# Convolution-attention hybrid, two layers: edge columns of a key-table group in one transfer, other ring sizes, new order offsets

## The chip, the cores and the metric

The kernel runs on one core of a Trainium2 chip. The core has TensorE (PE), whose weight loads are listed apart (PEld), VectorE (DVE), ScalarE (ACT), GpSimd (POOL), and SyncE (SP), which here only issues DMA transfers. The metric is the time of one execution on the device, in microseconds; smaller is better. Three runs of the kernel before took 1271.53 to 1274.23 us, with a median of 1273.8 us.

## The reference, cut to what matters

The input x has 2 images of 256 channels and 48x48 pixels. The first layer is a mixture of local attention and dynamic convolution:

```python
x = x + L0_conv(_gn(x))          # _gn: group norm
# in L0_conv, per image and per head (4 heads of 64 channels):
q = (Wq x + bq) * 64**-0.5 ; k = Wk x + bk ; v = Wv x + bv
uk, uv, upe = unfold 7x7 of k, v, pe, each padded by 3 with mode='reflect'
att = softmax(einsum('bdn,bdkn->bnk', q, uk + upe))
out_att = einsum('bnk,bdkn->bdn', att, uv)
# and two 3x3 depthwise convolutions with a relu between them
return rate1 * out_att + rate2 * out_conv
```

So each pixel attends to the 7x7 pixels around it, and at the border of the image the neighbours are reflected. The second layer (a state-space mixer and eight experts, two per token) follows on the same pixels as tokens. The change does not touch it.

## The kernel before, in words

Layer 0 runs for both images as one stream of work, and the second layer begins when it is done.

**Attention in blocks.** An image is cut into 18 blocks of 8x16 queries (`QR`, `QC`), six rows of three columns, 36 blocks in both images. A block needs the 14x22 keys around it (`KR`, `KC`, 308 in all). Its steps, with the lines of the profile: scores on PE (L811), mask and minimum on DVE (L827), exponentials on ACT (L838), transposes of the probabilities on PE (L846), their copy on ACT into a `pt` tile (L852), and the mix with the values on PE (L868). Beside that, DVE takes the inverse of each softmax sum (`rden`, L884). POOL widens it to a tile `rx` of 128x256 (L889), PE transposes that (L894), ACT copies the result from PSUM into a tile `rb` (L900), and DVE multiplies the mix with it (`ot`, L882, called norm here) and adds it to x (L878).

**Values through memory.** The values are computed in pairs of 128 pixels, nine pairs per image: product on PE (L749), copy on ACT into a `vout` tile (L756), store to a raster in device memory (L759). When three pairs are there, that is 16 rows of the image, the group is spread into a table, `vtab`, by transfers from memory to memory: for each of the three columns of blocks a strip of 22 pixels per row (L769), whose reflected edge columns come one by one, three at the left edge of the first strip (L772) and three at the right edge of the last (L775). For the top and bottom of the image three reflected rows are copied within the table (L781, L783, called ends here). A block then loads its 308 values of 256 channels in three transfers into a `val` tile (L911). All of these, stores, spreads, ends and loads, are issued by SP in one queue, in the order of the program: an issue that waits holds up all that stand behind it.

**Convolution beside it.** The two depthwise convolutions run in strips of 24 rows: most taps are multiply-adds on DVE (L565, L577), some are products on ACT (L626) which POOL adds by accumulating transfers (L638).

**Who sets the order.** Class `Flow` plans layer 0 as a list: every step has an engine, a cost in ns, the steps that it needs, and the ring slots that it takes and frees (`room`: two `vout`, three `val`, two `rb`, two `rx`, and so on). A step's rank is its due time less the length of what follows, less an offset of its kind from the table `LEAD0` (a minus or a plus behind the name stands for the first or the second half). Whenever an engine is free, the ready step of lowest rank with free slots is taken. The order found is the order of the instructions of PE, DVE, ACT and SP; POOL's follows it. The costs in the code only make the order. The engines wait for semaphores when they run.

Of the kernel before, what the change touches and what calls it, by code (L numbers as in the profile page):

```python
# [38 lines left out]
B, C, H, W = 2, 256, 48, 48  # L39
# [3 lines left out]
PAD = 3  # L43
HP = H + 2 * PAD
QR, QC = 8, 16
# [4 lines left out]
NRB, NCB = H // QR, W // QC  # L50
# [182 lines left out]
class Kernel:  # L233
# [104 lines left out]
    def layer0(self, ctx):  # L338


        nc, ins = self.nc, self.ins
        self.ps, self.used_banks = self.pool("ps", 1, ctx, space=bass.MemoryType.PSUM), []
        wts = self.pool("l0w", 1, ctx)
        room = dict(bank=2, banks=3, q=2, prob=3, pt=4, val=3, vout=2, hid=2, place=2, ct=2, cg=2, rb=2, ot=1, rx=2)
        self.begin_flow(self.pool("att", 1, ctx), room, self.PACE0, self.LEAD0, NBQ * self.PACE0)
        self.xp = {(b, h): wts.tile([P, H, W], F32, name=f"xp{b}{h}") for b in range(B) for h in range(NH)}
        self.kp = [wts.tile([P, HP, HP], F32, name=f"kp{h}") for h in range(NH)]
        self.prepare(wts)
        self.scale_weights()
        for b in range(B):  # L350
            self.group_norm(b)
            for g in range(-(-H // KG)):
                self.keys(b, g)
            for rb in range(NRB):
                self.queries(b, rb)
            for pair in range(N // (2 * P)):
                self.values(b, pair)
            self.convolutions(b)
            for i in range(NBQ):
                self.block(b * NBQ + i)  # L360
        self.run_flow()
# [371 lines left out]
    def values(self, b, pair):  # L733


        nc, T, p0 = self.nc, self.tiles, 2 * P * pair
        flat = [self.xp[b, h].rearrange("p r c -> p (r c)") for h in range(NH)]
        raster, key = self.vraster[b], (b, pair)
        r1 = (p0 + 2 * P) // W
        done = (p0 + 2 * P) % (VR * W) == 0  # L740
        group = p0 // (VR * W)
        c = b * NBQ + NCB * next(rb for rb in range(NRB) if min(QR * rb + QR + PAD, H) > group * VR)

        def product():
            ps = self.bank_for(("v", key))
            for i in range(2):
                p = p0 + i * P
                for k in range(NH):
                    nc.tensor.matmul(  # L749
                        ps[:, i * C : (i + 1) * C], lhsT=flat[k][:, p : p + P], rhs=self.l0["Wv"][:, k, :],  # L750
                        start=k == 0, stop=k == NH - 1,
                    )

        def copy():
            out = self.large_tile("vout", key, [P, 2, C])
            nc.scalar.copy(out.rearrange("p i c -> p (i c)"), T["bank", ("v", key)])  # L756

        def store():
            nc.sync.dma_start(raster[p0 : p0 + 2 * P, :].rearrange("(i p) c -> p i c", p=P), T["vout", key])  # L759

        def spread():
            r0 = r1 - VR
            src = raster.rearrange("(r c) d -> r c d", c=W)
            strips = self.vtab[b].rearrange("s (r c) d -> s r c d", c=KC)
            rows = slice(PAD + r0, PAD + r1)
            for cb in range(NCB):
                c0, c1 = max(0, cb * QC - PAD), min(W, (cb + 1) * QC + PAD)
                at = c0 - (cb * QC - PAD)
                nc.sync.dma_start(strips[cb, rows, at : at + c1 - c0, :], src[r0:r1, c0:c1, :])  # L769
                for j in range(PAD):  # L770
                    if cb == 0:
                        nc.sync.dma_start(strips[cb, rows, j : j + 1, :], src[r0:r1, PAD - j : PAD - j + 1, :])  # L772
                    if cb == NCB - 1:
                        col = QC + PAD + j
                        nc.sync.dma_start(strips[cb, rows, col : col + 1, :], src[r0:r1, W - 2 - j : W - 1 - j, :])  # L775

        def ends():
            strips = self.vtab[b].rearrange("s (r c) d -> s r c d", c=KC)
            for j in range(PAD):
                if group == 0:  # L780
                    nc.sync.dma_start(strips[:, j], strips[:, 2 * PAD - j])  # L781
                if r1 == H:
                    nc.sync.dma_start(strips[:, PAD + H + j], strips[:, PAD + H - 2 - j])  # L783

        self.op(c, ("v", key), "PE", 1730, product, *self.normalized(b, p0 // W, r1), ("wv1", 0), takes=[("bank", ("v", key))])
        self.op(c, ("vc", key), "ACT", 570, copy, ("v", key), takes=[("vout", key)], uses=[("bank", ("v", key))])
        self.op(c, ("vs", key), "queue", 4500, store, ("vc", key), uses=[("vout", key)])
        if done:
            self.op(c, ("vt", (b, group)), "queue", 10000, spread, *[("vs", (b, p)) for p in range(pair - 2, pair + 1)])
            if group == 0 or r1 == H:  # L790
                self.op(c, ("ve", (b, group)), "queue", 5800, ends, ("vt", (b, group)))

    def block(self, c):
# [122 lines left out]

    PACE0 = 8517
    LEAD0 = {
        "Wk-": -2983844, "Wq-": -2364428, "Wv-": 1379269, "add+": 4672699, "add-": -218998,
        "bkp-": -329119, "bq8-": -347513, "bv1-": -2824447, "c1+": -2744499, "c1-": 604148,  # L920
        "c2+": -3568598, "c2-": -4067744, "c3+": -4192745, "c3-": 1206176, "ca+": -316981,
        "ca-": 1533923, "cd+": -6915146, "cd-": 3124390, "copy+": 5626139, "copy-": -1580149,
        "cp+": -1382670, "cp-": -1157911, "cst-": 2506359, "exps+": -3895413, "exps-": -4687265,
        "g2+": 3892042, "g2-": -3058028, "ga-": -6766507, "gneg-": 557252, "gs-": -9485502,
        "ka+": -2261356, "ka-": 4495797, "kb+": 754107, "kb-": 2128455, "kk+": -355426, "kk-":
        95965, "least+": -852851, "least-": -3615547, "line-": -4892590, "mix+": 3379755,
        "mix-": 5352508, "norm+": -2808328, "norm-": -848702, "place+": 2730989, "place-":
        4548299, "q+": 272749, "q-": 1258423, "qp+": -359879, "qp-": 5581, "rc+": -1347439,
        "rc-": 1599623, "rden+": -1647488, "rden-": -463776, "relu+": 7308982, "relu-": 4577314,
        "row-": -5624948, "rstd-": 3924930, "rt+": 965921, "rt-": -18691, "rx+": -6558515,  # L930
        "rx-": -3369941, "score+": 3504231, "score-": 2190083, "sw+": -848532, "turn+":
        -1205935, "turn-": 84883, "v+": 110806, "v-": 10811, "val+": 448065, "val-": 3685159,
        "vc+": -519738, "vc-": -124400, "ve+": 2263088, "ve-": -7064210, "vec-": -4450165,
        "vs+": -1985565, "vs-": -5738649, "vt+": 5333280, "vt-": 1460046, "w2r-": -7510221,
        "win-": 4743570, "winw+": -1186160, "woutc+": 774295, "woutd+": 1826874, "woute+":
        -6026117, "woutt+": -512791, "woutw+": -8672401, "wp-": -1208524, "wv1-": -2064644,
        "x-": -4900900, "xp-": -8007513,
    }


# [1485 lines left out]
```

## Time and profile before

| what | us |
|---|---|
| median of three runs | 1273.8 |
| the profiled execution, its own time | 1275.69 |
| its span | 1273.9 |
| PE busy in the span | 1205.9 |
| DVE, ACT, POOL busy | 897.5, 779.9, 612.7 |
| end of layer 0 (last residual add of a block) | 304.6 |
| in 0 to 306: PE, DVE, ACT, POOL busy | 271.2, 261.9, 235.1, 127.1 |
| in 0 to 306: share of DMA engines busy | 0.65 |

The span is the time from the first to the last recorded instruction of one profiled execution. Busy time is the union of the records of an engine; matmuls are pipelined and their ends are modelled, so that a busy PE need not be at its peak. In a timeline a row is a group of like instructions that follow one another, with the idle time before the first and what released it. Rows of SP (`SPq`) are the issues of transfers, not the transfers themselves.

### The profile page before, as it was taken

To read this page: it belongs to the slowest core of one execution; us is meant where nothing else is said; L and a number is where in the kernel's file an instruction comes from. 1 tells how busy PE (TensorE), PEld (TensorE's weight loads), DVE (VectorE), ACT (ScalarE), POOL (GpSimd) and SP (SyncE) were. 2 spreads that over 40 slices of the span, in tenths; PEclk is the share of its full clock that TensorE was granted. 3 is DMA by queue.
4 is the path that set the end of the run, shared out by engine and by line. 5 is a ranking of instruction groups with operands and counts; after the bars stand their busy time and mean duration, and the time that the engine had idled before them with its cause. 6 is when DMAs were issued, how large, how long until landed. Compare 5 with 4: busy or idle time off the path is not lost. (4 is left out here: it accounts for less than half of the span.)

```text
span 1273.9 us, 23367 instructions
## 1 busy us (share of the span) xinstructions
PE 1205.9 (95%) x8024; PEld 977.0 (77%) x8024; DVE 897.5 (70%) x2385; ACT 779.9 (61%) x1774; POOL 612.7 (48%) x773
## 2 busy tenths in 40 slices
PE   4989999997999999999999989999999999999995
PEld 2666675776667777777776878999999999999995
DVE  7966899997687988888888645655555655556442
ACT  2488887997889888789698633333333333334342
POOL 3761235524367789899899872121212122212220
PEclk9989999998899999999999999999999999999998
DMA  7678873651223334335454248667657667656756
GB/s 261 157 191 217 207 182 76 140 127 42 74 88 99 103 100 129 123 96 174 140 180 143 69 135 273 186 229 228 221 173 257 186 227 221 229 174 216 224 180 211
DMA packets 106733, 212.98 MB, mean 167 GB/s; under 512 B 11615, under 2 KB 83632, under 8 KB 101680
## 3 DMA queue, kind: packets, MB, share of 16 engines
q1 hardware_dynamic: 85488, 168.51, 38.8%
q0 software_dynamic: 19008, 38.62, 16.0%
q10 hardware_dynamic: 2116, 4.33, 1.0%
q8 instruction: 65, 1.06, 0.3%
q14 instruction: 56, 0.46, 0.1%
HBM read 154.24 MB, written 43.23 MB: 155 GB/s over the span
## 5 line engine op out<-in xcount | busy, mean ns | idle before, releaser
L2154 POOL DMA_INDIRECT acc<-ey,token x70 | 109.3, 1562 | 367.6 <-ACT ey L2153 310.5
L2144 PE MATMUL bank<-ext,wt 128*128 128x256 f32 (+1 forms) x1152 | 241.3, 368 | 0.0
L2148 ACT ACTIVATE hid<-bank,bt 128x256 f32<-128x256 f32 (+1 forms) x288 | 132.1, 460 | 171.3 <-PE bank L2144 166.5
L2144 PEld LDWEIGHTS bank<-ext,wt 128*128 128x128 f32 x1152 | 207.0, 190 | 25.0
L2187 PE MATMUL po<-ts,ss 128*128 128x128 f32 x768 | 96.2, 275 | 0.0
L975 PE MATMUL bank<-xn,win 128*128 128x387 f32 x240 | 93.2, 512 | 1.6 <-ACT t L1058 1.6
L1188 DVE SCALAR_TENSOR_TENSOR xc<-bank,vec,xc 128x384 f32<-128x384 f32 x144 | 86.5, 610 | 8.4 <-ACT xc L1177 8.1
L2187 PEld LDWEIGHTS po<-ts,ss 128*128 128x128 f32 x768 | 90.9, 192 | 0.0
L1404 ACT ACTIVATE mt<-mt,cum 128x128 f32<-128x128 f32 x288 | 87.7, 392 | 0.0
L1738 POOL DMA_INDIRECT xs<-u,rows x72 | 73.2, 1016 | 17.5 <-issue 15.1
L838 ACT ACTIVATE prob<-prob,top 128x308 f32<-128x308 f32 x144 | 78.6, 556 | 3.5 <-DVE top L827 3.5
L2191 ACT COPY u<-po 128x128 f32<-128x128 f32 x32 | 8.5, 265 | 114.0 <-PE po L2187 114.0
L2131 DVE TENSOR_TENSOR ss<-hid 128x512 f32<-128x512 f32 x32 | 22.1, 691 | 70.6 <-ACT hid L2148 70.6
L975 PE MATMUL zbank<-xn,win 128*128 128x384 f32 x192 | 71.1, 492 | 0.3 <-ACT z L1306 0.3
L1510 PE MATMUL bank<-wout,y 128*128 128x264 f32 x288 | 70.3, 389 | 0.1
L565 DVE SCALAR_TENSOR_TENSOR hid<-xp,vec,hid 128x1175 f32<-128x1175 f32 (+1 forms) x48 | 69.9, 1457 | 0.1
L577 DVE SCALAR_TENSOR_TENSOR x<-hid,w2r,x 128x1128 f32<-128x1128 f32 (+1 forms) x48 | 66.8, 1396 | 1.3 <-ACT hid L569 0.9
L2187 PE MATMUL po<-wt,hid 128*128 128x128 f32 x496 | 65.5, 275 | 0.0
L889 POOL COPY rx<-rden 128x256 f32<-128x256 f32 x36 | 30.8, 858 | 70.9 <-DVE rden L884 59.2
L827 DVE CUSTOM_DVE_ANT_0 prob<-banks,cst 128x308 f32<-128x308 f32 x144 | 62.2, 471 | 2.4 <-PE banks L811 2.3
L846 PE MATMUL banks<-cst,prob 128*112 128x128 f32 x432 | 57.5, 276 | 4.4 <-ACT pt L852 2.6
L975 PEld LDWEIGHTS bank<-xn,win 128*128 128x128 f32 x240 | 42.6, 196 | 24.4 <-issue 4.2
(339 smaller groups left out, 3005.8 us busy)
## 6 DMA issues: line engine op xcount, KB each, us to landing
wt<-in_We SPq DMA_DIRECT2D x36, 2048.0 KB
mt<-decays SPq DMA_DIRECT2D x36, 512.0 KB
ex<-xs SPq DMA_DIRECT2D x36, 265.0 KB
rd<-decays SPq DMA_DIRECT2D x68, 128.0 KB
val<-vtab SPq DMA_DIRECT2D x72, 112.0 KB
bt<-in_We SPq DMA_DIRECT2D x36, 136.0 KB
hid<-ct POOLq DMA_DIRECT2D x8, 600.0 KB
vraster<-vout SPq DMA_DIRECT2D x18, 256.0 KB
```

The costliest lines, as they stand in the source:

```text
L565: nc.vector.scalar_tensor_tensor(dst, src, w[:, k : k + 1], dst, ALU.mult, ALU.add)
L577: nc.vector.scalar_tensor_tensor(dst, src, w[:, k : k + 1], dst, ALU.mult, ALU.add)
L838: nc.scalar.activation(t, t, AF.Exp, bias=T["top", c][:, a : a + 1], scale=-1.0, accum_out=T["den", c][:, a : a + 1])
L975: self.nc.tensor.matmul(ps, lhsT=lhs(k), rhs=rhs(k), start=k == 0, stop=k == NH - 1)
L1188: nc.vector.scalar_tensor_tensor(out(), T["bank", ("cv", at)][:, i : i + TB], wc[:, i : i + 1], out(), ALU.mult, ALU.add)
L1404: nc.scalar.activation(t, t, AF.Relu, bias=at_s, scale=-1.0)
L1510: nc.tensor.matmul(ps[:, : C + E], lhsT=T["y", c][:, m, :], rhs=self.l1["wout"][:, m, :], start=m == 0, stop=m == NZ - 1,)
L1738: ins = nc.gpsimd.indirect_dma_start(self.xs, bass.IndirectOffsetOnAxis(ap=of("rows")[:, i, q : q + 1], axis=0), T["u2", g][:, i, :], None,)
L2144: nc.tensor.matmul(ps[:, :rows], lhsT=w1[:, k, c * P : (c + 1) * P], rhs=xt[:, k, :], start=k == 0, stop=k == NH - 1,)
L2148: nc.scalar.activation(hid[:, c, :], ps[:, :rows], AF.Gelu, bias=bt[:, c : c + 1])
L2154: put = nc.gpsimd.indirect_dma_start(self.acc, bass.IndirectOffsetOnAxis(ap=token[:, j : j + 1], axis=0), y, None, compute_op=ALU.add)
L2187: nc.tensor.matmul(p[name], lhsT=v[a][:, c], rhs=v[w][:, c], start=c == 0, stop=c == NHC // 2 - 1)
```

## The change

1. In the spread of a value group the left and right edge columns are no longer issued apart. For each of the three offsets one transfer moves the column of the left edge and the column of the right edge: both access patterns get a leading dimension of two. Each group has then three strips and three edge transfers, nine issues before and six after.
2. `val` has four tiles instead of three, `rb` and `rx` have one each instead of two.
3. The planner's costs of a value store (4500 to 5200) and of a spread (10000 to 9000) are other numbers, and all offsets of `LEAD0` are new. These change the order of the instructions of layer 0 on every engine.

```diff
-        room = dict(bank=2, banks=3, q=2, prob=3, pt=4, val=3, vout=2, hid=2, place=2, ct=2, cg=2, rb=2, ot=1, rx=2)
+        room = dict(bank=2, banks=3, q=2, prob=3, pt=4, val=4, vout=2, hid=2, place=2, ct=2, cg=2, rb=1, ot=1, rx=1)
...
-                for j in range(PAD):
-                    if cb == 0:
-                        nc.sync.dma_start(strips[cb, rows, j : j + 1, :], src[r0:r1, PAD - j : PAD - j + 1, :])
-                    if cb == NCB - 1:
-                        col = QC + PAD + j
-                        nc.sync.dma_start(strips[cb, rows, col : col + 1, :], src[r0:r1, W - 2 - j : W - 1 - j, :])
+            for j in range(PAD):
+                to, of = strips[0:2, rows, j, :], src[r0:r1, PAD - j : PAD - j + 2, :].rearrange("r c d -> c r d")
+                (s, _), (c, _) = to.ap[0], of.ap[0]
+                to = bass.AP(to.tensor, to.offset, [[(NCB - 1) * s + (QC + PAD) * C, 2], *to.ap[1:]])
+                of = bass.AP(of.tensor, of.offset, [[(W - 2 - PAD) * c, 2], *of.ap[1:]])
+                nc.sync.dma_start(to, of)
...
-        self.op(c, ("vs", key), "queue", 4500, store, ("vc", key), uses=[("vout", key)])
+        self.op(c, ("vs", key), "queue", 5200, store, ("vc", key), uses=[("vout", key)])
...
-            self.op(c, ("vt", (b, group)), "queue", 10000, spread, *[("vs", (b, p)) for p in range(pair - 2, pair + 1)])
+            self.op(c, ("vt", (b, group)), "queue", 9000, spread, *[("vs", (b, p)) for p in range(pair - 2, pair + 1)])
...
     LEAD0 = {
-        "Wk-": -2983844, "Wq-": -2364428, "Wv-": 1379269, "add+": 4672699, "add-": -218998,
+        "Wk-": -2899864, "Wq-": -3041340, "Wv-": 482392, "add+": 4897790, "add-": -42794,
...
-        "vs+": -1985565, "vs-": -5738649, "vt+": 5333280, "vt-": 1460046, "w2r-": -7510221,
+        "vs+": -3334969, "vs-": -6382773, "vt+": 5829367, "vt-": 203986, "w2r-": -7681203,
...
```

## The prediction

> **What bounds the kernel now.** I read the chain that ended last first: its 28 pieces all lie after 1250.91 us, in the results, which the change does not touch. So I went by stages. Layer 0 ends at 304.6 us (the last residual add, L878); everything changed lies before it, and what layer 0 loses or gains moves the rest by as much. In the table of stages (columns: window; length; busy us of PE, PEld, DVE, ACT, POOL; clock; DMA share; GB/s):
>
> ```profile
> 20.00:48.00 28.00, 26.28 (x76) 13.96 (x77) 28.00 (x32) 9.80 (x11) 22.19 (x35) 1.00 0.47 143
> 48.00:75.00 27.00, 21.50 (x118) 14.03 (x116) 20.02 (x49) 19.52 (x38) 19.26 (x26) 0.95 0.83 208
> 75.00:175.00 100.00, 93.81 (x758) 71.60 (x756) 77.03 (x181) 88.31 (x190) 24.68 (x31) 0.96 0.80 203
> 175.00:295.00 120.00, 117.69 (x965) 83.30 (x964) 115.42 (x264) 107.46 (x247) 53.34 (x77) 1.00 0.54 121
> ```
>
> From 175 us PE, DVE and ACT are all at 90% or more: nothing to win there. Between 48 and 175 us PE stands idle 11.7 us, DVE 30 us, and the clock is below 1. Who PE waits for, in the timeline (start; busy us; engine and line; idle before and its releaser):
>
> ```profile
> 73.65 2.83 PE L868 MATMUL bank<-pt,val 84*64 84x128 f32 x24 [3.40 <-DMA val<-vtab]
> ...
> 117.19 0.87 PE L846 MATMUL banks<-cst,prob 128*112 128x128 f32 x6 [2.28 <-ACT pt L852]
> 117.90 0.38 PE L894 MATMUL bank<-cst,rx 128*128 128x128 f32 x2
> 118.83 0.41 PE L894 MATMUL bank<-cst,rx 128*128 128x128 f32 x2 [0.55 <-ACT vout L756]
> ...
> 153.16 0.41 PE L894 MATMUL bank<-cst,rx 128*128 128x128 f32 x2 [3.09 <-ACT vout L756]
> 153.41 0.82 PE L846 MATMUL banks<-cst,prob 128*112 128x128 f32 x6
> 154.16 2.82 PE L868 MATMUL bank<-pt,val 84*64 84x128 f32 x24
> ```
>
> The first product with the values waits 3.40 us for its load; the other two wait behind a value copy on ACT, and ACT's timeline says what that copy waits for:
>
> ```profile
> 115.86 0.58 ACT L756 COPY vout<-bank 128x512 f32<-128x512 f32 x1 [3.63 <-DMA vraster<-vout]
> 152.43 0.58 ACT L756 COPY vout<-bank 128x512 f32<-128x512 f32 x1 [4.21 <-DMA vraster<-vout]
> ```
>
> It wants one of two vout tiles, whose store has not landed, because SP issued it late. SP's queue at the second place:
>
> ```profile
> 141.06 1.96 SPq L769 DMA_DIRECT2D vtab<-vraster  x2
> 143.06 4.84 SPq L775 DMA_DIRECT2D vtab<-vraster  x3
> 148.00 5.40 SPq L759 DMA_DIRECT2D vraster<-vout  x3
> ```
>
> The value copy of pair 15 ends at 142.7, but SP is inside the previous group's spread until 147.9 and issues the store at 148.0. At 109.77 the same: the copy ends at 107.1, SP is still in the ends of the table (L783). And the first value load is issued at 68.51, behind 15 table issues.
>
> **What the skill says.** The Trainium skill, TensorE: Matmul & The Clock Gate, section "Why this matters for your kernels", warns of PE gaps over about 3 us, after which its clock drops. The trace agrees: after the gaps of 3.40 and 3.09 us the 24 products took 2.83 and 2.82 us, elsewhere 1.54, so each such gap costs 1.3 us more; after 2.28 + 0.55 us it does not. DMA: Bandwidth & Descriptors, section "Why a DMA increments its semaphore by 16 and not by 1", says that a transfer uses the largest number of engines up to 16 that divides both sides' slowest dimension. The old edge transfer is 16 rows (16 engines), the merged one is 2x16 (2 engines). No trace shows this yet. The same page, "Anatomy of one DMA", gives about 2.0 us fixed per transfer; here a store issued by 40.4 us released the spread at 42.29, which agrees.
>
> **The change part by part.**
> Merged edges. Six groups had six edge issues each, now three: 18 fewer of 0.588 us (median of L775), 1.8 us of SP's queue per group, 10.6 us in all. Bytes stay. Not on PE's path by itself; it lets what is queued behind it (stores, value loads, ends) go earlier. Against it, each transfer puts 16 packets on each of two engines. SP's queue moved 22512 packets in 29.4% of 16 engines' 306 us, 64 ns each: 1.0 us per transfer, 3.1 us for three in a row on these two, before a store queued behind lands. Only a copy that needs that store soon pays. In the new order the first spread is followed by stores 3 to 5, whose copies re-use vout; the last two stores also stand behind a spread, but no value copy follows. Bounds 0 and 4.4 us (3.1 and the clock); I take 1.0.
>
> Fourth value tile. A value load now waits for the mix four blocks back, not three. SP waited 91.8 us for L868 in 21 waits; whatever stood behind stood too. In the new order of SP every value load that waits for a mix stands ahead of stores whose products come after that mix on PE, so it holds no store up. From 175 us on PE hardly waits for values (one 0.2 us in the last 30 us): worth nothing there.
>
> New offsets move whole steps. Before, PE does six key products, then value pairs; after, three value pairs stand behind the first key product and six pairs stand ahead of the first query product. Adding up PE's instructions in order, by their durations here (key product 1.9 us, value pair 1.9, query 1.5, scores 1.3, turn 0.84, mix 1.54), the sixth pair ends after 20 us of PE work instead of 34, while the first mix starts after 50 instead of 48. So the first value loads, behind two spreads that can now be issued by about 50 us, are some 20 us ahead of the first mix; its 3.40 + 1.29 = 4.7 us go. This one I count in full.
>
> The two later stalls hold 2.83 and 3.09 + 1.28, together 7.2 us. Their causes go: the ends (L783) now stand ahead of the loads, well before the stores, and stores 14 and 15 ahead of the spread that held 15 up. But all orders differ, and ACT (88.31 of 100 us) and DVE must keep pace: in 75 to 175 us PE's remaining idle is other small waits which will come back elsewhere. I take 60%, 4.3 us. DVE has the room: in the new order six convolution steps of 1.4 us more stand before the 18th norm (65 against 59), work that fills the idle 30 us.
>
> What is paid. (a) Early value pairs push key products between DVE's convolution steps: following the two banks by hand, PE waits about 0.2 + 1.7 + 0.3 us for DVE's key adds against 1.6 in that stretch before: 0.6. (b) One rx tile: a widening (L889, 0.39 to 1.9 us, median 0.69) waits for the block before's transposes; behind it on POOL wait the accumulating DMA issues, and for those the convolutions. Consecutive transposes lie 2.8 us or more apart in the new order, so it fits: 0 to 2, I take 0.5. Below 0 it has no way. (c) One rb tile: ACT's copy (L900) waits for the norm before (L882, 0.42 us); two copies stand side by side only at the end of the stage: 0 to 0.6, I take 0.4. Together with the edges' 1.0: 2.5 us.
>
> Sum: 4.7 + 4.3 - 2.5 = 6.5 us. The profiled execution took 1275.69 us (1273.9 of span, 1.8 around it): 1269.2. The median of the three runs is 1273.8, 1.9 below it, so I say 1267.3.
>
> **Rivals.**
> All of it comes back: 11.9 us of stalls go and nothing is paid, 1261.9. For: each stall's cause is removed in the order itself, and the second half shows that three engines can run at 90 to 98% together. Against: half the waits in such an order turn up somewhere else.
> Nothing gained: ACT and the small rings set the pace of the first half, and the idle time moves into PE's waits for pt and prob (2.6 and 1.7 us now): 1273.5. For: ACT is at 88% from 75 us. Against: ACT's own longest waits there (3.63 and 4.21) are the ones removed.
> Slower: the two-engine edges. A spread's edges land late on two engines, stores and value loads queued behind land 3.1 us late, and PE stalls 3.1 + 1.3 = 4.4 us a time. One or two such stalls only eat the gain; from three groups of six it cancels (13.2 against 11.9), with four it is 17.6 - 11.9 = 5.7 us slower, 1279.5. For: DMA share is 0.80 to 0.83 there, so the two engines have no slack. Against: behind most spreads stand value loads with blocks of slack.
>
> **How the numbers follow.** Likeliest case 46%, its own range 1264 to 1270.5. All back 25%, 1260.5 to 1264. Nothing 16%, 1271 to 1276. Slower 13%. Within 0.2% means 1271.3 to 1276.3, about what a measurement of this kernel can tell from none. Faster: 46 + 25 and 3 of the third case, 74%; same 13 and 1 of the last, 14%; slower 12%. The range takes in the first three cases: 1260.5 to 1276.
>
> **What would show it.** Right: the first mix without a wait for val and taking 1.54; no value copy waiting over 1 us for a store; layer 0 ending near 298 us; DVE over 80% in 75 to 175 us; 18 edge issues of about 0.59. Wrong: waits for a landing behind L775; POOL waiting for L894 far over 7.2 us; PE idle of 16 us in the stage as before, only behind other releasers.

## The result, and the profile after

The kernel after takes 1266.96 us in the median, beside 1274.23 us for the kernel before on the same chip: a ratio of 0.9942, with a 95% interval of 0.9927 to 0.9957. The profiled execution has a span of 1264.9 us, 9.0 less than the one of before.

Not all of the 9.0 us is the change. The first key product (L702) starts at 17.57 us after and at 19.58 before; in the runs below it starts anywhere from 17.66 to 19.60, with either order. From there to the start of the last residual add (L878: 305.1 us before, 296.4 after) layer 0 takes 285.5 us before and 278.8 after: 6.7 us. What follows takes the same in both to 0.3 us. (The table of before lets layer 0 end at 304.6 us; that was misread, the last add starts at 305.1. No term of the prediction's sum uses it.)

The stages of the kernel after, in the columns of the table of before (window; length; busy us of PE, PEld, DVE, ACT, POOL; clock; DMA share; GB/s):

```profile
20.00:48.00 28.00, 24.74 (x85) 16.02 (x84) 24.38 (x31) 9.43 (x13) 18.80 (x26) 0.94 0.68 195
48.00:75.00 27.00, 26.75 (x147) 17.43 (x147) 25.76 (x62) 24.28 (x48) 19.32 (x26) 1.00 0.82 218
75.00:175.00 100.00, 94.48 (x740) 68.34 (x740) 81.35 (x177) 86.65 (x190) 36.80 (x58) 0.98 0.78 192
175.00:295.00 120.00, 118.36 (x1030) 85.11 (x1030) 115.95 (x274) 109.38 (x251) 44.77 (x62) 1.00 0.50 112
```

PE's idle time, length less busy time over these four windows, falls from 15.7 to 10.7 us. The other part is the clock that PE was granted, as a share of full speed. Windows of 5 us, in the same columns, show where it was low, in the kernel before:

```profile
70.00:75.00 5.00, 1.60 (x16) 1.35 (x16) 2.24 (x6) 1.95 (x3) 5.00 (x5) 0.73 0.91 232
75.00:80.00 5.00, 5.00 (x23) 3.36 (x22) 3.03 (x8) 2.99 (x5) 0.24 (x1) 0.59 0.95 221
...
150.00:155.00 5.00, 1.91 (x17) 1.69 (x18) 0.81 (x2) 2.57 (x8) 1.33 (x2) 0.92 0.59 159
155.00:160.00 5.00, 5.00 (x42) 3.75 (x40) 4.85 (x15) 4.80 (x13) 1.01 (x2) 0.74 1.01 255
```

and in the kernel after:

```profile
30.00:35.00 5.00, 2.65 (x7) 1.36 (x8) 5.00 (x5) 0.00 (x0) 4.75 (x6) 0.97 0.58 204
35.00:40.00 5.00, 5.00 (x18) 4.12 (x17) 5.00 (x7) 0.87 (x2) 4.93 (x10) 0.69 0.49 101
...
95.00:100.00 5.00, 1.00 (x4) 0.71 (x5) 1.08 (x4) 3.15 (x6) 1.94 (x3) 0.96 0.89 210
100.00:105.00 5.00, 5.00 (x37) 3.74 (x36) 1.35 (x8) 3.57 (x15) 0.18 (x1) 0.70 0.99 236
```

One less the clock (the column third from the end), times the length, is 3.4 + 1.7 us before and 1.7 + 1.7 after. In windows of 1 us the first spell of before runs at 0.50 from 72.3 to 79.1 us, of which PE was busy from 73.65: 2.7 us lost. So the clock took 4.4 us before and 3.4 after, 1.0 less, and with the 5.0 us of idle time 6.0 of the 6.7 us are placed. The gain lies between 48 and 80 us, where PE's idle time to 75 us goes from 5.5 to 0.25 us and a slow spell goes too. Between 20 and 48 us PE lost 1.5 us and some clock, and between 75 and 175 it won only 0.7 us of idle time.

Where PE stands in the timeline of the kernel after (start; busy us; instruction; idle before and its releaser):

```profile
34.23 7.13 PE L749 MATMUL bank<-Wv,xp 128*128 128x256 f32 x24 [2.19 <-DVE kp L708]
...
69.50 1.54 PE L868 MATMUL bank<-pt,val 84*64 84x128 f32 x24
...
97.58 0.41 PE L894 MATMUL bank<-cst,rx 128*128 128x128 f32 x2 [2.76 <-ACT vout L756]
...
99.41 3.67 PE L749 MATMUL bank<-Wv,xp 128*128 128x256 f32 x8 [1.42 <-DVE ot L882]
...
116.60 0.44 PE L894 MATMUL bank<-cst,rx 128*128 128x128 f32 x2 [0.56 <-POOL rx L889]
```

The first mix (69.50) waits for nothing and takes 1.54 us instead of 2.83 after a wait of 3.40. The stalls at 117 and 153 us of before are gone. A new one stands at 97 to 99 us, with the mechanism of the old ones: transposes behind a value copy on ACT that wants a vout tile. ACT's timeline, and SP's queue ahead of it:

```profile
96.85 0.59 ACT L756 COPY vout<-bank 128x512 f32<-128x512 f32 x1 [4.40 <-DMA vraster<-vout]
```

```profile
72.59 3.17 SPq L775 DMA_DIRECT2D vtab<-vraster  x3
75.80 3.71 SPq L911 DMA_DIRECT2D val<-vtab  x3
83.47 2.61 SPq L783 DMA_DIRECT2D vtab<-vtab  x3
86.13 6.78 SPq L911 DMA_DIRECT2D val<-vtab  x6
93.02 4.80 SPq L759 DMA_DIRECT2D vraster<-vout  x3
```

The copy of pair 9 ends at 85.9 us, but its store is only issued at 93.02: ahead of it stand the lower ends of image 1 (L783), which wait 3.8 us for the third spread to land, and the six issues of two value loads, which take 6.78 us.

### The profile page after: what moved, and what is told of

Its sections match the earlier page's. It is cut to its first block, busy times and chain, and to the rows that moved or that the text cites. A ratio compares the mean times of both kernels' runs of the same rounds, so it can differ in the third digit from the quotient of the medians.

```text
span 1264.9 us, 23341 instructions
## 1 busy us (share of the span) xinstructions
PE 1204.7 (95%) x8024; PEld 975.4 (77%) x8024; DVE 897.8 (71%) x2385; ACT 780.2 (62%) x1774; POOL 611.2 (48%) x773
## 5 line engine op out<-in xcount | busy, mean ns | idle before, releaser
L1510 PEld LDWEIGHTS bank<-wout,y 128*128 128x128 f32 x288 | 53.0, 192 | 9.9 <-issue 1.1
L2187 PEld LDWEIGHTS po<-wt,hid 128*128 128x128 f32 x496 | 60.3, 192 | 0.0
```

The lines of the kernel that those rows point to most:

```text
L1510: nc.tensor.matmul(ps[:, : C + E], lhsT=T["y", c][:, m, :], rhs=self.l1["wout"][:, m, :], start=m == 0, stop=m == NZ - 1,)
L2187: nc.tensor.matmul(p[name], lhsT=v[a][:, c], rhs=v[w][:, c], start=c == 0, stop=c == NHC // 2 - 1)
```

## The experiments

All are ratios to the kernel before, run beside it on one chip; its median was 1276.8, 1276.7, 1273.5 and 1276.3 us in the four groups. "Layer 0" is the time from the first key product to the last residual add, and "waits" the sum of the waits that PE's timeline lists in that time (0.17 us and longer), both in one profiled execution.

| kernel | median us | ratio, 95% interval | layer 0, us | waits, us |
|---|---|---|---|---|
| before | | 1 | 285.5 | 15.5 |
| after | 1266.96 | 0.9942 (0.9927 to 0.9957) | 278.8 | 10.3 |
| before_edges | 1274.91 | 0.9985 (0.9971 to 0.9999) | 289.1 | 18.8 |
| after_edges16 | 1267.94 | 0.9931 (0.9912 to 0.9950) | 278.5 | 10.3 |
| after_old_edges | 1267.70 | 0.9925 (0.9907 to 0.9942) | 278.4 | 9.6 |
| before_moves | 1268.91 | 0.9939 (0.9921 to 0.9957) | 277.8 | 9.6 |
| before_first | 1272.14 | 0.9966 (0.9953 to 0.9979) | 279.9 | 10.1 |
| before_stores | 1271.66 | 0.9959 (0.9945 to 0.9973) | 279.1 | 9.5 |
| before_offsets | 1291.22 | 1.0118 (1.0092 to 1.0143) | 298.8 | 25.6 |
| after_ends | 1268.75 | 0.9946 (0.9927 to 0.9965) | 280.2 | 12.6 |
| after_val3 | 1264.85 | 0.9935 (0.9914 to 0.9957) | 276.7 | 10.0 |
| before_room | 1291.61 | 1.0137 (1.0112 to 1.0163) | 305.5 | 29.0 |
| before_moves_edges | 1267.92 | 0.9954 (0.9938 to 0.9970) | 279.3 | 9.7 |
| after_val3_old_edges | 1266.64 | 0.9920 (0.9899 to 0.9941) | 279.0 | 10.8 |

One profiled execution is not the median: the one of before_edges lies 8.8 us above its kernel's median. So verdicts rest on the ratios, and profiles are read for where waits stand.

### Do the edge columns matter?

The expectations of these runs set theories against each other. A: the issues that SP saves are time won. B: a merged transfer, on two engines, lands late. C: the load of all engines makes landings late.

Three kernels: the kernel before with merged edges alone; the kernel after with the pair of columns as the second dimension of the transfer, so that 16 rows are its slowest; the kernel after with the six separate edge columns of before.

before_edges takes the new loop of the change's diff into the kernel before, after_old_edges the old loop into the kernel after, and after_edges16 is the kernel after with:

```diff
-                to = bass.AP(to.tensor, to.offset, [[(NCB - 1) * s + (QC + PAD) * C, 2], *to.ap[1:]])
-                of = bass.AP(of.tensor, of.offset, [[(W - 2 - PAD) * c, 2], *of.ap[1:]])
+                to = bass.AP(to.tensor, to.offset, [to.ap[1], [(NCB - 1) * s + (QC + PAD) * C, 2], *to.ap[2:]])
+                of = bass.AP(of.tensor, of.offset, [of.ap[1], [(W - 2 - PAD) * c, 2], *of.ap[2:]])
```

> The kernel before with the merged edge transfers alone; offsets, rings and order as before. Theory A (SP's queue is freed: 18 issues of 0.588 us fewer, so stores and value loads behind a spread go 1.8 us earlier per group): 1 to 3 us faster, 1271 to 1273, the two waits of a value copy for a store (3.63 and 4.21 us) shorter by 1 to 2 us each. Theory B (a merged transfer runs on two DMA engines and lands late): the gain on SP's queue is eaten by waits for the landing before the ends of the table (L781, L783), 0 to 4 us slower, 1274 to 1278, and SP waits for vtab<-vraster over 5 us in all against 1.0 before.

> The changed kernel with the rows as the leading dimension of the merged edge transfers (16 x 2 x 256 instead of 2 x 16 x 256); all else the same. Theory B (the two-engine transfers land late): SP's waits for vtab<-vraster before the ends, 10.7 us in the changed kernel, fall to about 1 us, the value copy at 96.85 us no longer waits 4.40 us, PE's 2.76 + 1.42 us behind it go, and the time falls by 2 to 5 us to 1262 to 1265. Theory C (it is the load of all DMA engines, near 0.8, that makes landings late): nothing changes, 1266 to 1268.

> The changed kernel with the six separate edge transfers of before; order of everything else, rings and offsets as changed. Theory A (the 1.8 us of SP's queue per group count): 1 to 4 us slower, 1268 to 1271. Theory B (two-engine landing is what costs): landings are short again, so it is no slower and perhaps 1 to 3 us faster, 1264 to 1267, with SP's waits for vtab<-vraster near 1 us.

The counts of SP's queue between 0 and 306 us (packets, MB, share of 16 engines) in the kernels before, after and after_edges16, in this order:

```profile
q1 hardware_dynamic: 22512, 29.74, 29.4%
```

```profile
q1 hardware_dynamic: 21972, 29.73, 29.6%
```

```profile
q1 hardware_dynamic: 22224, 29.73, 30.2%
```

The Trainium skill, DMA: Bandwidth & Descriptors, section "Why a DMA increments its semaphore by 16 and not by 1", says that each engine that takes part in a transfer ends with a write to the semaphore. The counts fit: 36 transfers of 16 rows and 16 such writes are 1152 packets, 18 of 32 rows and 2 writes are 612, 540 fewer, and 18 of 32 rows and 16 writes are 864, 288 fewer. These are the differences measured. So the merged transfer does run on 2 engines.

In time hardly a difference shows. The three forms in the kernel after have 0.9942, 0.9931 and 0.9925, with intervals that overlap widely. In the kernel before merged edges give 0.15%, with an interval that nearly reaches 1, and added to the three moves below nothing. The two value copies that theory A wanted to wait less wait 4.83 and 4.13 us for a store in the profile of before_edges, 3.63 and 4.21 in the kernel before. The stall near 98 us is there with all three forms, on 16 engines a shorter one (1.47 us, beside 2.76 after and 2.70 with old edges).

SP's waits for a spread to land before it issues the ends (L781, L783) do differ: 10.7 us in all in the kernel after, 6.9 on 16 engines, 3.3 with old edges and 0.5 in the kernel before. So in these single profiles two engines account for 3.8 us of them, and none of that shows in the time. What becomes of the shorter issue is seen at the third spread, counted from the first key product: the last issue of its edges ends at 58.2 us in the kernel after and 61.7 with old edges, but the ends, which wait for the landing, are issued at 65.9 and 65.4 (64.3 on 16 engines). The time that SP saved in issuing it spent waiting for the landing.

### Is it the order of SP's queue?

If the three stalls of the kernel before come from what stands ahead of a late issue, moving those issues alone must give the gain. before_moves is the kernel before with three steps held back; PE, ACT, DVE and POOL keep their orders. before_first has the first of the moves alone, before_stores the other two.

```diff
+HELD, LATER = {}, {("vt", (0, 1)): ("val", 0), ("ve", (0, 2)): ("vs", (1, 2)), ("vt", (1, 1)): ("vs", (1, 7))}
+def later(key, make): return (lambda: HELD.__setitem__(LATER[key], make)) if key in LATER else make
+def then(key, make): return lambda: (make(), HELD.pop(key, lambda: None)())
...
-        self.op(c, ("vs", key), "queue", 4500, store, ("vc", key), uses=[("vout", key)])
+        self.op(c, ("vs", key), "queue", 4500, then(("vs", key), store), ("vc", key), uses=[("vout", key)])
...
-                self.op(c, ("ve", (b, group)), "queue", 5800, ends, ("vt", (b, group)))
+                self.op(c, ("ve", (b, group)), "queue", 5800, later(("ve", (b, group)), ends), ("vt", (b, group)))
```

The spread and the first value load are wrapped in the same way.

> The kernel before with three moves in SP's queue alone and nothing else: the first value load ahead of the second spread, the lower ends of image 1 behind the stores 9 to 11, the second spread of image 2 behind the stores 15 and 16. Theory of the prediction (the three PE stalls of 3.40, 2.83 and 3.09 us, and the clock after two of them, 11.9 us in all, come from where SP's queue stands): the three stalls go, 7 to 11 us faster, 1263 to 1267, as much as the whole change. Rival (waits come back elsewhere, because ACT, DVE and the rings set the pace): the named stalls go but others take their place, 0 to 3 us faster, 1271 to 1274.

> The kernel before with one of the three moves alone: SP issues the first value load ahead of the second group's spread instead of behind it. Theory (each move is worth the stall that it removes, and the moves are independent): the first mix starts without its wait of 3.40 us and takes 1.54 us instead of 2.83, 4.7 us less, so about 1272 where the kernel before takes 1276.8; the two stalls at some 117 and 153 us stay as they were. Rival (the first blocks run ahead of a slower supply, so that a stall removed at the start is met again at the next late store): 0 to 2 us less, and the stalls at 117 and 153 us grow. Rival of sum: the whole gain of the three moves (7.9 us) comes from this one.

> The kernel before with the other two moves alone: the lower ends of image 1 behind the stores of pairs 9 to 11, and the second spread of image 2 behind the stores of pairs 15 and 16. Theory of independent moves: the stalls of 2.83 and 3.09 + 1.28 us go, the first mix still waits 3.4 us and takes 2.83; 7.2 us less at most, about 3 to 6 us after what comes back (the run with all three moves gained 7.9 of 11.9), so 1271 to 1274. Rival (the rest of the order refills the gaps): less than 2 us.

PE's timeline of before_moves at the first mix and at the largest waits left:

```profile
70.38 1.54 PE L868 MATMUL bank<-pt,val 84*64 84x128 f32 x24
...
142.82 0.41 PE L894 MATMUL bank<-cst,rx 128*128 128x128 f32 x2 [1.39 <-ACT vout L756]
...
171.90 2.92 PE L868 MATMUL bank<-pt,val 84*64 84x128 f32 x48 [1.94 <-DMA val<-vtab]
```

Of before_first:

```profile
66.28 1.54 PE L868 MATMUL bank<-pt,val 84*64 84x128 f32 x24
...
109.59 1.52 PE L846 MATMUL banks<-cst,prob 128*112 128x128 f32 x6 [2.32 <-ACT pt L852]
...
145.57 0.41 PE L894 MATMUL bank<-cst,rx 128*128 128x128 f32 x2 [2.57 <-ACT vout L756]
```

Of before_stores:

```profile
69.37 0.92 PE L868 MATMUL bank<-pt,val 84*64 84x128 f32 x8 [2.21 <-DMA val<-vtab]
```

Each move takes away its own stall and leaves the others where they were: before_first keeps the waits of 2.32 and 2.57 us (2.28 and 3.09 in the kernel before), and before_stores keeps the wait of the first mix. The later moves also bring a new wait for values: 1.94 us near 172 us in before_moves and 2.26 near 174 in before_stores, where before_first has 0.20. The first is worth 0.34% or 4.3 us (2.7 to 6.0), the other two 0.41% or 5.2 us (3.4 to 7.0). Together they give 0.61% or 7.8 us, less than the sum of 9.5 but within the intervals. So a kernel with old rings, old edges and old offsets, and three steps of SP moved, is as fast as the whole change.

before_moves_edges adds the merged edges to the three moves; a combination that could beat both kernels.

> The kernel before with the three moves in SP's queue and the merged edge columns together. The three moves alone took 1268.9, the edges alone 1274.9. What PE still waits for behind SP with the three moves is 1.39 us for a copy that wants a store, near 143 us, and 1.94 us for a value load behind the last spread, near 172 us, whose 48 products then take longer. If each spread shorter by 1.8 us of issue brings what stands behind it forward by as much: both waits go, 2 to 4 us less, 1265 to 1267, faster than the kernel after or the same. If edges on two engines land later than they are issued earlier, or the waits move: 1268 to 1271.

It has 0.9954, no better than the moves alone. The waits at 143 and 172 us are gone, and PE's timeline has one of 2.89 us for pt at 170.42 in their place.

### Does the kernel after gain by another such move?

In after_ends the lower ends of image 1 stand behind the stores of pairs 9 to 11.

```diff
+HELD, LATER = {}, {("ve", (0, 2)): ("vs", (1, 2))}
```

> The kernel after, with one move in SP's queue: the lower ends of image 1 (three issues that copy rows within the table) stand behind the stores of pairs 9 to 11 instead of ahead of them. Theory (in the kernel after too, what is left of the stalls is a store held in SP's queue behind issues that wait for a landing): ACT's copy of pair 11 waits less than 1 us instead of 4.40, PE's stalls of 2.76 and 1.42 us near 98 us go and the value product behind them takes 1.9 instead of 3.67 us, together up to 6 us less, half of it kept: 1262 to 1265 where the kernel after takes 1267. Rival (the order around has no room: the wait moves to the next store, or to the value loads of the last row of blocks, which now wait for the later ends): 1266 to 1269.

The theory fell in time: 0.9946, no better than the kernel after. The copy of pair 11 waits 1.50 us instead of 4.40 and PE's wait of 2.76 us is gone, but PE's timeline of after_ends has other waits:

```profile
67.26 2.67 PE L702 MATMUL bank<-xp,Wk 128*128 128x480 f32 x4 [2.05 <-ACT vout L756]
...
98.88 1.99 PE L749 MATMUL bank<-Wv,xp 128*128 128x256 f32 x8 [1.32 <-DVE ot L882]
...
130.85 1.32 PE L811 MATMUL banks<-kp,q 64*128 64x308 f32 x8 [2.48 <-ACT pt L852]
```

The first and the last are not in the profile of after. The first lies before the moved issues, so it is no effect of the move. With one profile of each it stays open how much of the others is.

### Rings and offsets

before_offsets is the kernel before with the new offsets and costs, before_room is the kernel before with the new rings. after_val3 has three value tiles; the planner then gives the same order to PE, DVE, ACT and POOL, and two value loads stand elsewhere in SP's queue. after_val3_old_edges is that with the six old edge columns; from before_offsets it differs in `rb` and `rx` alone.

```diff
-        room = dict(bank=2, banks=3, q=2, prob=3, pt=4, val=4, vout=2, hid=2, place=2, ct=2, cg=2, rb=1, ot=1, rx=1)
+        room = dict(bank=2, banks=3, q=2, prob=3, pt=4, val=3, vout=2, hid=2, place=2, ct=2, cg=2, rb=1, ot=1, rx=1)
```

> The kernel before with the new offsets and the two new costs only: three val, two rb and two rx tiles and single edge columns stay. If the order is what pays and the ring sizes only make it possible by chance: within 2 us of the whole change, 1266 to 1270 where the kernel before takes 1276.8, with the first mix free of a wait for val. If the fourth val tile is what lets the value loads stand far enough ahead: 1272 or more, and waits of PE for val between 70 and 175 us. The offsets were chosen for the new rings, so a worse order (over 1277) is also possible; then the two parts only work together.

> The kernel before with the new ring sizes alone (val four tiles, rb and rx one each), its own offsets and single edge columns. The planner gives other orders for it (484 lines of PE's order differ). The run with the new offsets and the old rings took 14.5 us more than the kernel before. If the offsets were fitted to the rings, the old offsets with the new rings are also slower than before: 1280 or more, and the gain of the whole change belongs to neither part alone. If the fourth val tile is the gain: 1270 or less. If single rx and rb tiles only cost what the prediction gave (0.5 and 0.4 us): within 2 us of before's 1276.7.

> The kernel after with three value tiles instead of four. The orders of PE, DVE, ACT and POOL stay word for word; in SP's queue two value loads stand in other places (the fifth behind a store instead of ahead of two of them, the last but one behind the lower ends of image 2), and a load can be under way only three blocks ahead. If the fourth tile is worth nothing (the prediction's step): within 2 us of the kernel after, 1265 to 1269, and PE's stalls near 98 us get smaller, since one load fewer stands ahead of stores 10 and 11. If the fourth tile is what keeps the values off PE's path: waits of PE for val after 70 us, 3 to 8 us slower, 1270 or more.

> The kernel after with three value tiles and with six separate edge columns: of the change only the offsets, the two costs and the single rb and rx tiles are left. It is the kernel of the run with the new offsets and old rings, with rb and rx at one tile each and nothing else different. If the gain of the whole change is the order that the new offsets give with these two rings, and neither the fourth value tile nor the merged edges add to it: a ratio to the kernel before of 0.991 to 0.995, as the kernel after has (0.9942) and the one with three value tiles (0.9935). If the merged edges are needed once the tile is gone (three tiles let the loads go later, so that SP's queue is tighter): 0.997 or more. Against the run with rb and rx at two tiles (1.0118) it is some 22 us less for an order that the planner changes when two ring sizes are other numbers.

The new offsets with the old rings are 1.2% slower than before, the old offsets with the new rings 1.4%. Only together are they faster. What the ring sizes change is the planner's order: with two `rb` and `rx` tiles or one, under the same offsets, PE's timelines in before_offsets and after_val3_old_edges follow different orders from 73 us on. In before_offsets it is not one stall. DVE's waits between 175 and 320 us there (tile and line; who it waits for; us in total, times, longest):

```profile
DVE ot L882 <- ACT rb L900: 14.8, 11, 3.4
DVE rden L884 <- ACT prob L838: 5.5, 5, 2.5
```

In the kernel after these two were 1.1 and 0.8 us between 175 and 300. DVE's norms then come late, and PE is busy 107 of the 120 us from 175 on, where it was 118. In before_room the largest wait is the old mechanism at its worst, on ACT and in SP's queue:

```profile
161.70 0.59 ACT L756 COPY vout<-bank 128x512 f32<-128x512 f32 x1 [11.10 <-DMA vraster<-vout]
```

```profile
150.62 2.68 SPq L775 DMA_DIRECT2D vtab<-vraster  x3
153.40 1.39 SPq L911 DMA_DIRECT2D val<-vtab  x3
154.83 2.06 SPq L781 DMA_DIRECT2D vtab<-vtab  x3
157.00 5.68 SPq L759 DMA_DIRECT2D vraster<-vout  x3
```

PE waits 10.17 us behind that copy. The store stands behind a spread, a value load and the ends.

The fourth value tile is worth nothing: 0.9935 with three, and in that profile PE's wait at 97 us is missing. ACT's timeline of after_val3:

```profile
93.94 0.58 ACT L756 COPY vout<-bank 128x512 f32<-128x512 f32 x1 [1.08 <-DMA vraster<-vout]
```

With old edges and three tiles it is back, in PE's timeline of after_val3_old_edges:

```profile
99.12 0.41 PE L894 MATMUL bank<-cst,rx 128*128 128x128 f32 x2 [2.52 <-ACT vout L756]
```

and yet that kernel has 0.9920, the lowest ratio of all. Its interval overlaps that of the kernel after, so it is not shown to be faster. It shows that offsets, costs and single `rb` and `rx` tiles hold the whole gain. More vout tiles, and the old `rb` and `rx` beside four value tiles, were not tried.

## Why the prediction was right

The forecast was 1267.3 us, the time is 1266.96, and the stalls did come from SP's queue. But four of its terms were off by 1 us or more.

**First mix, 4.7 us in full.** Right in kind: no wait and 1.54 us. In the two profiles it is worth more, since the low clock behind the wait lasted to 79 us and took 2.7 us, of which only what the 24 products showed (1.29) was counted: 6.1 us. The kernel before with this one move won 4.3 us in the median, and its interval holds 4.7 as well. (Ahead of the first value load stood 21 table issues, not 15: two spreads and one set of ends. No term uses that number.)

**The two later stalls, 60% of 7.2 us.** The old stalls went. The reason given, that every value load waiting for a mix stands ahead of stores whose products come later, and the ends well ahead of the stores, was not enough: it looked at what a load waits for on PE and left out what the issues wait for in landing. Ends that waited 3.8 us and loads that took 6.78 us to issue held store 9 until 93.02. So "no value copy waiting over 1 us for a store" was wrong, 4.40 us. The old stalls held 2.83 + 3.09 us and 1.7 of clock, 7.6; the new one holds 2.76 + 1.42 and 1.7, 5.9. So in the two profiles this term is 1.7 us, not 4.3.

**Edges on two engines, 1.0 us, and the rival built on them.** The layout is as read, the cost isn't there: 16 engines and separate columns give the same time within some 0.2%. The sign given for it, waits for a landing behind L775, did appear (SP's ends waited 10.7 us for the spreads to land, in five waits). On 16 engines they still waited 6.9, so two engines are at most a part of the cause, and that part did not show in the time. The 18 issues took 0.589 us in the median, as said.

**Key products between DVE's steps, 0.6 us.** Under-sized. PE waits 2.19 + 0.40 us for the key adds and 0.67 for `q`, beside some 1.6 us before, and in this profile the clock fell behind the first of these (1.7 us: 24 value products in 7.13 us). That is 3.4 us paid, half of it by chance: behind 2.15 us in after_edges16 the same products took 5.70.

**One rx tile, 0.5 us.** Right in size, and the sign named against it was a bad one. POOL's wait for PE's transposes went from 7.2 to 30.2 us, far over the bound, and PE waited for rx once, 0.56 us. POOL was waiting for something else before (59.2 us for DVE's `rden`, 17.4 after): one wait took the place of another on an engine that sets no pace.

**One rb tile, 0.4 us.** No wait of ACT for a norm is listed. **Fourth value tile, nothing:** right, by the run with three.

**The sum** of the two profiles is so 6.1 + 1.7 - 3.4, and 1.7 for PE's other listed waits, which fell where the prediction had 1.9 us of cost for edges, rx and rb: 6.2 us before rounding, against 6.5 predicted and 6.7 measured. That the total came so close is luck: terms that were off both ways cancelled.

**The signs.** Layer 0 ending near 298 us: 296.8, with 2.0 us of that won by an earlier start. DVE over 80% in 75 to 175 us: 81.35. PE idle of 16 us in the stage: 10.7.

Of the rivals, "nothing gained" would be 0.9998 and lies outside the interval, as does "slower". "All of it comes back" would be 0.9907 and lies outside too: three stalls of 11.9 us went, and 6.7 to 7.8 us stayed with either order.

What is shown is that the three stalls were made by the order of SP's queue and are worth 0.6% (0.43 to 0.79) in the kernel before. That they are the gain of the kernel after is argued from its profile: its order differs on all engines, and one part of it cannot be taken over without the rest. Open is also why the stall near 98 us appears in four profiles of that order (after, after_edges16, after_old_edges, after_val3_old_edges) and is small in the ones of after_val3 and after_ends, without the times telling these kernels apart.

## What to carry to other kernels

When one queue issues everything, read a stall back through it: which buffer, which store, what stood ahead of it and what was that waiting for; then move the one step, and take landings into account as well as the work that a step waits for. A table of order offsets is worth only what it gives with the ring sizes beside it, so neither is judged alone. A merged transfer that saves issue time gained nothing here, where the next step waits for the landing anyway.

## What was not expected of the hardware

The Trainium skill, TensorE: Matmul & The Clock Gate, section "Why this matters for your kernels", gives gaps over about 3 us as what lowers the clock. Here the length of a gap didn't decide alone: 24 value products took 7.13 us behind one of 2.19 us in the kernel after, and 5.70 behind one of 2.15 in after_edges16. Six transposes (L846), 0.87 us elsewhere, took 1.52 us behind 2.32 us in before_first, but 0.87 behind 2.28 us in the kernel before, and behind 2.65 us in before_edges, where the clock fell only 1.9 us after they began. The gap of 3.48 us in before_offsets doubled them (1.85 us), as the page has it.

The traces show what else decides. Windows of 1 us in which the clock falls, two of the kernel before and two of the kernel after (the clock is again third from the end):

```profile
72.00:73.00 1.00, 0.00 (x0) 0.00 (x0) 0.24 (x1) 0.00 (x0) 1.00 (x1) 0.64 0.88 254
154.00:155.00 1.00, 1.00 (x11) 0.84 (x10) 0.81 (x2) 1.00 (x4) 0.47 (x1) 0.60 1.08 213
...
34.00:35.00 1.00, 0.78 (x3) 0.68 (x4) 1.00 (x2) 0.00 (x0) 1.00 (x2) 0.85 0.15 54
99.00:100.00 1.00, 0.59 (x2) 0.51 (x3) 1.00 (x4) 1.00 (x3) 1.00 (x2) 0.78 0.84 214
```

The clock is 1.00 before and 0.50 after the fall, so it fell at 72.28 and 154.20 us, and at 34.70 and 99.56. In the same way it rose at 79.12 and 157.62, and at 38.12 and 102.96. All these times lie whole steps of 3.41 us apart: 2, 22 and 1 steps in the kernel before, 1, 18 and 1 in the kernel after. In the other twelve profiles every change in layer 0 lies on such a grid too, each profile with a grid of its own position.

The clock fell at the end of steps in which PE was busy only a little: 1.38 and 1.05 of 3.41 us in the kernel before, 1.22 and 0.57 in the kernel after. It did not fall where the old waits near 117 us were spread over two steps, with 1.66 and 2.33 us busy. It rose at the end of a step in which PE was busy throughout; at the first mix the first slow step had only 2.06 us of work, so a second one followed, and the spell took 2.7 us of busy time instead of 1.7. No sharp limit shows: a step of 1.45 us in before_room stayed fast, and one of 1.89 us in before_moves did not. So what a gap of 2 to 3 us costs depends on where it falls on the grid, which differs from one profile to the next; that part of a profile's time is chance.
